# A written-out order of some 3,300 pieces of work laid out anew on one core: pairwise attention, sparse gathers and layernorms

## The chip, the cores and the metric

The kernel runs on one core of a Trainium2 chip. The metric is the device time of one execution in microseconds (us), lower is better. Each of the core's engines (PE for matmuls, DVE for vectors, ACT for functions, POOL for gathers, SP for the other transfers) works through its own list of instructions strictly in the order in which the kernel emits them, and waits where an instruction needs another engine's result.

## The reference

All sizes are 3327 nodes by 256 features, float32. `adj` is sparse (each entry is there with probability 0.0024, and the diagonal always).

```python
h = relu(layernorm(x))
# layer 0, two steps
R = adj + eye;  R = R / R.sum(-1, keepdims=True)
Z = 0;  Xf = Xa = h
for n in range(2):
    A  = top_p_attention(Xa, W1, W2, W3)       # softmax(q k^T), the largest until 0.9 of the mass, renormalised
    Xf = R @ Xf
    Xa = A @ Xa
    Z  = Z + Xf @ U1[n].T + Xa @ U2[n].T
x = x + layernorm(h + Z) * ln_g + ln_b
# layer 1
h = relu(layernorm(x))
D = (adj.sum(1) + 1e-9) ** -0.5
x = x + relu((D[:, None] * adj * D[None, :] @ h) @ W.T + b)
```

## The kernel before

**Blocks and stages.** The nodes lie in 26 blocks of 128 rows, the last with 127. A start stage normalises all nodes, and makes keys, queries and the products of h with the weights, which it stores in HBM (`gb_hbm`). Then follow step 0 (`ATT_0`, `LISTING`, `FIRST`), step 1 (`ATT_1`, `SECOND`) and the late layer (`LATE`, `WHOLE`).

**A block of attention** (kinds `ATT_0`, `ATT_1`) goes over all 3327 columns: logits on PE (`lg0`, `lg1`, L866), exponentials on ACT (`ex0`, `ex1`, L883), then a search for the threshold by small steps and whole passes on ACT (`guess`, `ev1s`, `ev2s`, L897, L927), or for the first block or two by DVE (`w_over`, L934), set by `BY_VECTOR`. DVE then takes a window of the candidates (`win`, L1049), finds the largest of each stretch (`wm`, L1056), sorts the best 40 (`sort`, L1066 and L1069: MAX8, then MATCH_VALUE_LOAD and MATCH_REPLACE8, ten times), finds the cut, in step 1 marks the kept ones (`match`, L1109), and drops all others (`drop`, L1114). PE transposes the result in seven groups (`tr`, L1128), ACT copies them (`atc`, L1134), and PE multiplies them with the nodes (`att`, L1143). In step 0 `attend` (L1149), `xtk_t`, `xtk_c`, `k_m` and `k_c` (L814) then make the block's share of the keys of step 1; a step's first attention needs the keys of all blocks of the step before. In step 1 the block ends with residuals, two layernorms and the store of hn (`resid`, `input2`, `node2`, `stn`; L1254, L1258, L1273, L1288).

**Sparse products.** `LISTING` finds, for each block of rows, the nodes that its part of adj names, and lays the places of their columns into `a_idx` (L667) and their numbers into `v_idx`. From these POOL gathers 8 tiles of adj (`ga`, L678) and 8 tiles of nodes (`gv`, L692) by indirect DMA, each 128 rows; PE multiplies tile by tile (`adj0` to `adj7`, `adj_gathered`, L702). In step 0 (`FIRST`) the nodes come from gb_hbm and the products give y; in step 1 (`SECOND`) from y_hbm and give hz, which lies in HBM until the block's residual. In the late layer 18 blocks (`LATE`) gather 8 tiles of hn each, and 8 blocks (`WHOLE`: 0, 4, 7, 10, 13, 16, 19, 22) are done densely with 26 matmuls (L1554) in a part `first` and a part `second`: 25 and 1 for blocks 0 and 4, 13 and 13 for the others. In all POOL issues 768 gathers: 416 in step 0, 208 in step 1, 144 late.

**Buffers.** The gathered nodes go to 16 tiles in a ring: `gather_node` takes the tile that has been free longest, `adj_gathered` gives it back behind its matmul. There are 4 tiles for gathered adj, 3 for the attention's rows (`e`) and 2 for hz.

**What sets the order.** Nothing is scheduled by a compiler. Each piece of work (an `att2`, a `gv5`, a `sort3`) gets a number, and `Plan.run` emits the pieces sorted by it:

```python
places = PLACES[kind] | MOVED.get((kind, i), {})
at = BASES[kind] + PERIODS[kind] * (i if n is None else n) + (SHIFTS[kind][i] if kind < len(SHIFTS) else 0.0)
for name, piece in do.items():
    plan.add(at + places[name], piece)
```

The numbers are written by hand or by an earlier search. They look like times but are only sort keys: an engine starts each instruction as soon as the one ahead of it allows and what it reads is there. `PLACES` holds the places of one kind's pieces within a block, `PERIODS` the distance from block to block, `MOVED` a block's own places, and `EVENTS` the places of single pieces (the centring of the keys: `keys` for step 0, `centre` for step 1).

Of the kernel before, what the change touches and what calls it, by code (L numbers as in the profile page):

```python
# [105 lines left out]
BASES = (-1.892, 870.475, -13.053, -5.69, 853.823, -80.36, 1720.169, 1724.788)  # L106
PERIODS = (30.0573, 29.8334, 30.2195, 29.6001, 29.4593, 1.6, 11.4611, 29.3857)
# [11 lines left out]
        ldq=-44.287, lg0=-38.973, ex0=-25.597, lg1=-20.538, ex1=-16.452, guess0=-16.41, guess1=-16.131,  # L119
        guess2=-15.977, guess3=-15.603, guess4=-14.457, guess5=-14.33, guess6=-12.806, guess7=-12.277, ev1r=-11.76,  # L120
        ev1s=-8.469, st10=-7.961, guess8=-7.057, st11=-6.906, st12=-5.943, st13=-4.39, st14=-3.503, st15=-3.334,
        st16=-1.613, st17=0.027, thr=0.214, st18=0.892, win=3.72, cut0=7.309, wm1=9.04, wm0=10.134, wm3=10.495,
        wm2=12.344, sort0=14.201, sort1=14.201, sort2=15.126, sort3=16.348, sort4=16.684, sort5=17.022, sort6=18.245,
        sort7=18.909, sort8=19.469, sort9=19.668, cut1=19.862, cut2=20.795, cut3=21.407, cut4=22.022, cut5=22.834,
        drop=23.642, tr0=26.604, atc0=29.007, tr2=31.084, att0=32.223, atc2=32.504, tr1=33.541, atc1=35.266,
        inv=37.184, tr3=38.707, att1=40.1, tr4=41.126, atc3=41.825, att2=42.068, tr5=43.428, atc4=44.771,
        atc5=46.924, att3=47.519, tr6=48.685, atc6=50.691, att4=50.866, att5=51.309, edge=51.319, att6=52.006,
        attend=54.3, xtk_t=56.039, xtk_c=58.125, k_m=61.105, cut6=61.775, k_c=62.744, q_c=63.484, xu_m=65.976,
        xu_c=67.312, stxt=75.943, stq=77.565, stxu=81.473,
    ),  # L130
    dict(
        ldq=-120.275, lg0=-63.07, lg1=-47.295, ex0=-46.566, ex1=-41.634, guess0=-41.061, guess1=-39.487,
        guess2=-38.859, guess3=-38.65, guess4=-38.64, guess5=-37.462, guess6=-37.063, ev1s=-36.233, half=-35.672,
        mass0=-35.413, ev1r=-35.055, mass1=-32.043, tail0=-31.473, tail1=-31.053, tail2=-30.763, tail3=-28.525,
        mass2=-28.221, st10=-26.599, st11=-25.175, st12=-24.135, aux2=-23.815, ev2s=-21.461, st13=-18.043,
        btw1=-17.852, st14=-15.208, aux0=-14.988, aux1=-14.22, sec10=-12.922, sec11=-12.131, sec12=-10.743,
        thr=-7.89, sec13=-7.788, nt2=-2.992, win=2.783, wm2=6.046, wm0=6.444, wm1=6.454, wm3=6.526, sort0=8.121,
        sort1=8.162, sort2=9.437, sort3=10.527, sort4=11.217, sort5=12.023, sort6=12.773, sort7=13.564, sort8=15.249,
        cut0=15.328, sort9=15.348, cut1=16.458, cut2=17.341, cut3=18.102, cut4=18.886, cut5=19.961, match=21.123,
        drop=23.999, tr0=28.827, atc0=29.172, tr4=29.605, tr1=32.779, att0=32.801, tr2=32.803, atc1=33.007,  # L140
        att1=33.809, atc4=34.739, tr3=34.759, atc2=36.727, att2=37.933, tr5=38.539, tr6=39.45, atc3=40.18,
        att3=40.29, ldx=44.319, atc5=45.361, atc6=45.991, ldh=48.128, att4=48.571, inv=49.727, att5=50.339,
        att6=51.666, resid0=55.38, resid1=57.694, resid2=60.354, root1=64.136, xbet=66.296, input20=67.759,
        input21=69.483, edge=70.892, input22=73.309, input23=75.045, root2=79.569, node2=90.831, stn=94.821,
    ),
# [7 lines left out]
        store=12.996,  # L153
# [1634 lines left out]
```

## Time and profile before

| what | value |
|---|---|
| median of 11 runs | 1647.92 us (1646.08 to 1651.88) |
| the profiled execution's own time | 1650.14 us |
| its span | 1648.4 us |
| mean granted TensorE clock | 0.966 |
| PE busy | 1487.4 us (90%) |
| DVE busy | 1300.0 us (79%) |
| ACT busy | 1137.7 us (69%) |
| POOL busy | 1039.0 us (63%) |
| first gather starts | 95.56 us |
| last gather of step 0 starts | 771.45 us |
| first window of step 1 starts | 811.21 us |
| last drop of step 1 starts | 1421.91 us |
| first and last gather of hn start | 1450.38 and 1629.75 us |

The span is the time from the first to the last instruction on the chip. An engine's share is over the whole span. A row of a timeline has the start in us, the duration, the engine, the line of the kernel, the operation, what it writes and reads, and in brackets how long the engine stood idle ahead of it and what released it; "issue" means that nothing which the profile shows was waited for.

### The profile page before, as it was taken

How to read it: one execution, taken by the hardware profiler on the slowest of the kernel's cores; microseconds unless marked ns; L12 is line 12 of the kernel's file. 1: busy time of each engine (PE TensorE's matmuls, PEld its weight loads, DVE VectorE, ACT ScalarE, POOL GpSimd, SP SyncE). 2: the span in 40 equal slices, each digit the busy share in tenths (PEclk: the TensorE clock that was granted, in tenths of full speed). 3: DMA queues.
4: the chain of work that ended last, by engine and by line, in shares of the span. 5: the costliest groups of instructions: out<-in, count | busy, mean ns of one | idle time of the engine just before them, and what ended most of it. 6: DMA issues, size and time to landing. Idle time of an engine off the chain costs nothing.

```text
span 1648.4 us, 24872 instructions
## 1 busy us (share of the span) xinstructions
PE 1487.4 (90%) x7372; PEld 1161.8 (70%) x7372; DVE 1300.0 (79%) x3965; ACT 1137.7 (69%) x2692; POOL 1039.0 (63%) x808
## 2 busy tenths in 40 slices
PE   5958999989999999999499999999999998899996
PEld 3526777767777777777277777777777777788884
DVE  5589999779999997964599999999999999611111
ACT  3666887657777776872889999999999997200000
POOL 0058888788888887885566454566666562067774
PEclk9969999989999999999699999999999999999998
DMA  6556867657557766444533432343344334377764
GB/s 189 171 182 206 266 209 229 187 174 227 171 170 219 220 196 182 151 143 128 183 102 117 128 116 87 119 128 111 100 125 128 114 116 134 98 236 267 264 196 120
DMA packets 149167, 272.26 MB, mean 165 GB/s; under 512 B 29603, under 2 KB 94496, under 8 KB 148000
## 3 DMA queue, kind: packets, MB, share of 16 engines
q1 hardware_dynamic: 109456, 181.58, 33.8%
q0 software_dynamic: 33536, 87.08, 19.0%
q10 hardware_dynamic: 6032, 1.93, 0.5%
q8 instruction: 60, 0.98, 0.2%
q14 instruction: 83, 0.68, 0.1%
HBM read 221.08 MB, written 49.41 MB: 164 GB/s over the span
## 4 chain that ended last, share of the span: by engine, by line
PE 37%; DVE 27%; issue 11%; ACT 10%; DMA 6%; POOL 3%; SPq 0%; DVEq 0%; POOLq 0%; ACTq 0%
PE att_acc L1143 13%; DVE cand L1056 6%; DVE w L1109 5%; PE late_sums L1554 5%; PE adj_acc L702 4%; PE p_t L1128 4%; PE p_l L866 4%; PE late_acc L702 3%; DVE e L1114 3%; ACT e L883 3%; ACT ja L927 2%; DMA vg<-hn_hbm,v_idx 2%; DMA vg<-gb_hbm,v_idx 2%; DVE cand L1069 2%; DVE val L1066 2%
## 5 line engine op out<-in xcount | busy, mean ns | idle before, releaser
L692 POOL DMA_INDIRECT vg<-y_hbm,v_idx x208 | 326.1, 1568 | 254.0 <-PE adj_acc L702 192.0
L927 ACT ACTIVATE ja<-e,t 128x3327 uint8<-128x3327 f32 x127 | 389.6, 3068 | 0.7
L678 POOL DMA_INDIRECT ac<-in_adj_t,a_idx x208 | 276.5, 1329 | 146.9 <-DVE own L619 83.8
L1143 PE MATMUL att_acc<-h,at 128*128 128x256 f32 (+1 forms) x1352 | 323.6, 386 | 0.0
L1143 PE MATMUL att_acc<-xa,at 128*128 128x256 f32 (+1 forms) x1352 | 321.8, 382 | 0.0
L692 POOL DMA_INDIRECT vg<-gb_hbm,v_idx x208 | 273.9, 1317 | 63.4 <-issue 45.4
L1143 PEld LDWEIGHTS att_acc<-h,at 128*128 128x128 f32 (+1 forms) x1352 | 253.3, 193 | 40.7 <-issue 7.6
L1143 PEld LDWEIGHTS att_acc<-xa,at 128*128 128x128 f32 (+1 forms) x1352 | 253.2, 192 | 31.2
L1134 ACT COPY at<-p_t 128x512 f32<-128x512 f32 (+1 forms) x364 | 197.1, 545 | 110.7 <-PE p_t L1128 104.5
L1128 PE MATMUL p_t<-ident,e 128*128 128x128 f32 x1352 | 211.8, 283 | 51.8 <-DVE e L1114 38.0
L1128 PEld LDWEIGHTS p_t<-ident,e 128*128 128x128 f32 x1352 | 164.4, 145 | 110.7 <-DVE e L1114 41.1
L1056 DVE MAX8 cand<-w 128x8 f32<-128x208 f32 x832 | 238.6, 359 | 0.2
L702 PE MATMUL adj_acc<-vg,ac 128*128 128x257 f32 (+1 forms) x832 | 231.1, 391 | 8.5 <-DMA vg<-gb_hbm,v_idx 5.7
L866 PE MATMUL p_l<-kt,q 64*128 64x512 f32 (+1 forms) x832 | 183.7, 556 | 30.1 <-ACT e L883 28.0
L1049 DVE SCALAR_TENSOR_TENSOR w<-e,t 128x3327 f32<-128x3327 f32 x52 | 191.1, 3675 | 21.3 <-ACT t L897 21.0
L883 ACT ACTIVATE e<-p_l 128x2048 f32<-128x2048 f32 x104 | 161.6, 1554 | 18.2 <-PE p_l L866 15.9
L702 PEld LDWEIGHTS adj_acc<-vg,ac 128*128 128x128 f32 x832 | 149.3, 193 | 34.0 <-issue 8.3
L692 POOL DMA_INDIRECT vg<-hn_hbm,v_idx x144 | 136.5, 948 | 54.9 <-issue 36.7
L866 PEld LDWEIGHTS p_l<-kt,q 64*128 64x128 f32 x832 | 75.1, 193 | 113.3 <-issue 67.4
L730 ACT COPY xt_k<-p_turn 128x256 f32<-128x256 f32 x52 | 19.0, 369 | 152.8 <-PE p_turn L726 151.3
L570 DVE TENSOR_REDUCE most<-adj_sb 128x7 f32<-128x896 f32 x104 | 105.2, 1012 | 6.3 <-DMA adj_sb<-in_adj_t 5.4
L1114 DVE SCALAR_TENSOR_TENSOR e<-w,kept,e 128x3327 f32<-128x3327 f32 x26 | 96.7, 3719 | 0.1
(397 smaller groups left out, 2102.2 us busy)
## 6 DMA issues: line engine op xcount, KB each, us to landing
ac<-ac_hbm SPq DMA_DIRECT2D x70, 512.0 KB
adj_sb<-in_adj_t SPq DMA_DIRECT2D x78, 448.0 KB
ac_hbm<-ac SPq DMA_DIRECT2D x26, 512.0 KB
adj_row<-in_adj_t SPq DMA_DIRECT2D x8, 1664.0 KB
adj_sb<-in_adj_t SPq DMA_DIRECT2D x26, 320.0 KB
gb_hbm<-gb SPq DMA_DIRECT2D x26, 256.0 KB
gb<-gb_hbm SPq DMA_DIRECT2D x26, 256.0 KB
q<-q_hbm SPq DMA_DIRECT2D x104, 32.0 KB
```

Of the source, the lines that this page charges most:

```text
L678: nc.gpsimd.indirect_dma_start(s["list"][:, k, :], None, adj_rows, bass.IndirectOffsetOnAxis(ap=s["a_idx"][:, k : k + 1], axis=0))
L692: nc.gpsimd.indirect_dma_start(t[:, :D], None, hbm[:, :], bass.IndirectOffsetOnAxis(ap=v_idx[:, i, k : k + 1], axis=0))
L702: nc.tensor.matmul(s["acc"][:, :width], s["ac"][:, k, :], rows[:, :width], start=(k == 0), stop=(k == SLOTS - 1))
L866: nc.tensor.matmul(pl[:, at : at + cw], s["q"][rows, :], kt[rows, c0 + c : c0 + c + cw], start=True, stop=True)
L883: nc.scalar.activation(halves(s["e"])[:, :, c0 : c0 + w], logits_of(s.pop(("l", g)))[:, :, :w], AF.Exp, accum_out=s["zp"][:, g : g + 1],)
L927: nc.scalar.activation(junk, s["e"][:, :N], f, bias=s["t"], scale=-1.0, accum_out=s[name])
L1049: nc.vector.scalar_tensor_tensor(w[:, :N], ev, s["t"], ev, op0=ALU.is_le, op1=ALU.mult, accum_out=s["below"])
L1056: nc.vector.max(s["cand"][:, 8 * n : 8 * n + 8], s["w"][:, c0 : c0 + cw])
L1114: nc.vector.scalar_tensor_tensor(ev, kept, kept8[:, step * NB + i, 0:1], ev, op0=op, op1=ALU.mult, accum_out=den)
L1128: nc.tensor.transpose(pt[:, c : c + P], s["e"][:, b * P : (b + 1) * P], ident)
L1134: nc.scalar.copy(at[:, :w], pt[:, :w])
L1143: nc.tensor.matmul(s["att"][:, :D], at[:kb, c : c + P], v[b][:kb, :D], start=(b == 0), stop=(b == NB - 1))
```

## The change

Only the numbers of the order change. All instructions stay; they are emitted in another sequence. `PLACES` and `SHIFTS` are new throughout, and the first and last blocks of each step (0, 1, 25 of step 0; 0, 1, 2, 25 of step 1), some blocks of `FIRST`, `SECOND` and `LATE`, and all of `WHOLE` have places of their own in `MOVED`. In step 0 gathers of adj and of nodes take turns in shorter runs, and the products of `FIRST` lie later by about a block against the attention. In step 1 more of a block's sorting stands in one piece on DVE. In the late layer block 2 is gathered ahead of block 1, with their products in the old sequence. Two functions read a value one `yield` later, since a piece that writes it now may come after.

```diff
-BASES = (-1.892, 870.475, -13.053, -5.69, 853.823, -80.36, 1720.169, 1724.788)
-PERIODS = (30.0573, 29.8334, 30.2195, 29.6001, 29.4593, 1.6, 11.4611, 29.3857)
+BASES = (-1.219, 870.817, -13.308, 19.745, 850.288, -80.36, 1723.434, 1717.681)
+PERIODS = (30.0457, 29.8979, 30.2735, 28.5613, 29.0638, 1.6, 11.5234, 30.9119)
 ATT_0, ATT_1, LISTING, FIRST, SECOND, START, LATE, WHOLE = range(8)
...
-        gv3=36.873, gv6=37.71, gv1=38.549, gv0=39.478, gv5=41.654, gv2=42.696, lda=49.308, ldg=49.654, gv4=49.849,
-        gv7=50.182, adj0=50.797, adj1=50.94, adj2=53.03, adj3=56.206, adj4=57.968, adj5=59.203, adj6=62.128,
-        adj7=63.299, roots=65.636, prop=66.557, mixy=74.549, stxf=84.692,
+        gv1=5.282, gv2=21.832, gv7=24.204, gv6=26.685, lda=38.398, gv0=42.53, gv3=45.834, gv5=49.994, adj0=53.488,
+        gv4=54.175, adj1=54.407, adj2=56.475, adj3=58.925, ldg=60.866, adj4=61.154, adj5=61.417, adj6=63.064,
+        adj7=64.895, prop=68.892, roots=69.299, mixy=79.436, stxf=81.479,
...
     (6, 1): dict(
-        load=-179.07, gath=0.428,
+        load=-105.361, gath=8.668,
     ),
     (6, 2): dict(
-        load=-69.885, gath=9.897,
+        load=-54.284, gath=-3.365,
     ),
...
     (7, 7): dict(
-        row=-166.823, first=-44.325, second=-34.048, m=-27.848, turn=-18.413, mt=-15.792, out=-14.297, ldx=-2.972,
-        add=13.779, st=17.888,
+        row=-174.561, first=-143.338, second=-36.982, ldx=-23.235, m=-22.339, turn=-7.269, mt=-2.182, out=-1.77,
+        add=4.041, st=35.074,
     ),
...
 EVENTS = dict(
-    keys=-32.591, centre=764.748, roots=817.644, hn=827.229, nodes=878.278, last_nodes=918.935, hn_last=1606.3,
+    keys=-34.222, hn=759.96, centre=779.44, nodes=800.108, roots=866.959, last_nodes=881.044, hn_last=1387.109,
 )
...
     def step_0(s):
+        rest = fma("rest", s["z"], 1.0 - TOP_P, s["over"])
+        yield
         sign = s["sign"]
-        rest = fma("rest", s["z"], 1.0 - TOP_P, s["over"])
-        yield
         below = fma("below_n", sign, -0.5, value[AIM[0] - 0.5 * N])
...
     def input_2(i, t):
-        hz, x, n = t["hz"], t["x"], t["n"]
+        hz, n = t["hz"], t["n"]
         nc.vector.scalar_tensor_tensor(hz, hz, n["mv"][:, 0:1], gam, op0=ALU.subtract, op1=ALU.mult)
         yield
+        x = t["x"]
         nc.vector.scalar_tensor_tensor(x, hz, n["rr"], x, op0=ALU.mult, op1=ALU.add)
```

## The prediction, made before the changed kernel ran

> **What bounds the kernel now.** I read the windows first, because the whole-span shares mix three stages with three different limits. Columns: window, its length, then busy time and instructions of PE, PEld, DVE, ACT, POOL, and the granted clock, DMA share and GB/s.
>
> ```profile
> 600.00:630.00 30.00, 28.79 (x151) 22.91 (x149) 21.62 (x75) 23.13 (x55) 24.45 (x19) 1.00 0.66 210
> 780.00:810.00 30.00, 17.02 (x72) 10.30 (x70) 9.53 (x17) 24.95 (x59) 15.79 (x12) 0.78 0.48 153
> 990.00:1020.00 30.00, 27.76 (x141) 22.27 (x139) 29.58 (x81) 28.47 (x67) 11.37 (x13) 1.00 0.35 104
> 1590.00:1620.00 30.00, 28.80 (x138) 24.43 (x137) 6.68 (x15) 2.60 (x7) 22.69 (x25) 1.00 0.62 189
> ```
>
> POOL's 24.45 looks like room, but 19 gathers have 0.30 us of issue ahead of each: 24.45 + 19 x 0.30 = 30.2. In step 0 POOL never rests. The last row is the same case: 22.69 + 25 x 0.30 = 30.2. In step 1 (third row) DVE is full and POOL is not. Between steps (second row) nothing is full: there one chain of short steps sets the time.
>
> The timeline of POOL and DVE shows what a gather costs:
>
> ```profile
> 757.43 0.95 POOL L692 DMA_INDIRECT vg<-gb_hbm,v_idx  x1 [0.30 <-PE att_acc L1143]
> 758.68 3.71 POOL L692 DMA_INDIRECT vg<-gb_hbm,v_idx  x1 [0.30 <-issue]
> ...
> 757.88 3.68 DVE L1114 SCALAR_TENSOR_TENSOR e<-e,kept 128x3327 f32<-128x3327 f32 x1
> ```
>
> A gather's pitch is 0.95 + 0.30 = 1.25, but one that meets a 3.7 us DVE instruction (w_over, window, drop) stays until that ends. From 95.6 to 772.4 the trace holds step 0's 416 gathers with no gap over 0.45: 416 x 1.25 = 520, and 53 long ones add 154, sum 674, against 676.8 elapsed. The 53 are 26 windows, 26 drops and one w_over.
>
> Between the steps:
>
> ```profile
> 766.09 1.23 PE L702 MATMUL adj_acc<-vg,ac 128*128 128x257 f32 x2 [2.79 <-DMA vg<-gb_hbm,v_idx]
> ...
> 784.74 0.47 ACT L1149 ACTIVATE xa<-att_acc,inv 128x256 f32<-128x256 f32 x1 [2.46 <-PE att_acc L1143]
> 787.40 0.36 ACT L814 ACTIVATE kt<-p_kq,km 64x127 f32<-64x127 f32 x1
> ...
> 811.21 3.67 DVE L1049 SCALAR_TENSOR_TENSOR w<-e,t 128x3327 f32<-128x3327 f32 x1
> ```
>
> Block 25's drop ends at 761.5. PE then stands before FIRST(24)'s last product, for a gather; FIRST(25) lies among block 25's att matmuls. The last keys (kt) are there at 787.4, and 23.8 later step 1's first window starts.
>
> **The change, part by part.** Both kernels issue the same instructions; only their order on each engine differs, so the sum is one of waits. It is made against the profiled execution (1650.14; span 1648.4 and 1.7 around it), 2.2 above the median of the runs.
>
> *Start.* The first gather (95.56) waits for a_idx(0) on DVE. In the new order four chunk reductions lie between the centring of the keys and a_idx(0), before it one. Three more at 1.01 (L570's mean) cost 3.0, less about 0.4 because part lay elsewhere ahead of it: +2.6 (0 to +4).
>
> *Step 0.* The runs are shorter (369 runs of one kind instead of 306), but POOL's work is the same 520 + 154: as many gathers, and as many long DVE instructions. An in-order queue that is never idle gains nothing from order. PE's pauses here are slack beside POOL. It could lose if a gather found no free tile of 16; by the new order each tile comes free over 10 us ahead of its next gather. 0.
>
> *Between the steps.* FIRST(24)'s products now stand between att3 and att6 of block 25, and FIRST(25)'s behind (1,0)'s second logit group. So PE transposes as soon as the drop ends (761.5) and does 26 x 2 att records at 0.2165 (11.3), 26 transposes at 0.108 (2.8) and 8 products (3.5), 17.6 in all, to about 779 to 780 instead of 784.6; FIRST(25)'s three small ACT instructions (0.7) leave the path to kt. Worked through, kt comes near 780: -7.5, from 0 (another gather ends last) to -14 (no copy on ACT is waited for). y(25) is stored later, but y gathers have 231 us of gaps in step 1.
>
> *Step 1.* DVE is the bound, so its order has a price. The timeline of block 25's sorting shows it:
>
> ```profile
> 1414.16 0.29 DVE L1066 MAX8 val<-cand 128x8 f32<-128x128 f32 x1
> 1414.38 0.14 DVE L1103 TENSOR_TENSOR edge<-pre,thr 128x1 f32<-128x1 f32 x1
> ...
> 1414.88 0.29 DVE L1066 MAX8 val<-cand 128x8 f32<-128x128 f32 x1
> 1415.21 0.09 DVE L1069 MATCH_VALUE_LOAD cand<-val,cand 128x8 f32 x1
> 1415.29 0.28 DVE L1069 MATCH_REPLACE8 cand<-val,cand 128x128 f32<-128x128 f32 x1
> 1415.48 0.42 DVE L442 BATCH_NORM_STATS2 bn_st<-x_in 128x6 f32<-128x256 f32 x1
> ```
>
> A MAX8 whose next neighbour reads its output holds that neighbour back 0.33; with another instruction between, 0.22. Fitted over all pitches of step 1, a dependent neighbour costs 0.117. The old order has 134 such pairs from the first window of step 1 to its last match, the new one 231: the sorts run more in one piece, no longer between other blocks' small steps. 97 x 0.117 = +11.3, less 2.7 for pairs two apart: DVE's floor rises from 602.3 to 611.3. The old stretch took 610.5, so it held 8.2 of waits. If the new order has none, +0.8; with the same waits, +9. I take +6.8, nearer the upper end, because the rows with waits (t from ACT, L897) have no shorter path in the new order.
>
> The Trainium skill weighs against this term. Its page "VectorE: DVE Perf Modes", section "The DRAIN you can't avoid", says that after every DVE instruction the next starts only when the pipe is empty, whether or not the two are chained. By that, order would cost nothing and this term would be 0 or less; the rows' 0.22 against 0.33 say otherwise.
>
> *End of step 1.* Block 7's first dense part (13 matmuls, 5.6) now stands on PE just ahead of block 25's transposes. Of its 5.6, 2.4 fill the pause that PE has there (1425.74) and some 1.1 smaller pauses ahead of it; up to +2.1 is left, and hz's last load lies better by 1.5: +0.6 (-1.5 to +2.1).
>
> *Late layer.* Rows, with S = 1450.38 the first hn gather:
>
> ```profile
> 1450.38 0.96 POOL L692 DMA_INDIRECT vg<-hn_hbm,v_idx  x1 [11.07 <-issue]
> ...
> 1510.56 0.95 POOL L692 DMA_INDIRECT vg<-hn_hbm,v_idx  x1 [0.30 <-issue]
> ...
> 1508.27 3.62 PE L702 MATMUL late_acc<-vg,ac 128*128 128x256 f32 x16
> ...
> 1629.75 0.95 POOL L692 DMA_INDIRECT vg<-hn_hbm,v_idx  x1 [0.30 <-issue]
> ```
>
> 144 gathers at 1.252 reach to 1630.7 without a gap. Gather 49 (block 9's first, 1510.56) takes the tile that block 6's first product frees, and that product starts at 1508.27: in time by under 2. In the new order block 2 is gathered before block 1, but PE still multiplies block 1 first, so PE stands until gather 16 has landed: issued at S + 15 x 1.252 = S + 18.8, ended 0.95 later, landed 2.45 after its issue-end (766.09 against 763.64 above), S + 22.2; product done S + 22.6 instead of S + 15.7. From there to block 6's product PE has five dense halves (D7, D10, D13, D10, D13: 28.2), products 2, 3, 5 (10.4), D0's last matmul (0.4), and turns and outputs (6.1): 45.1, so S + 67.7, its first pair S + 68.1. Gather 49 is due at S + 60.1: POOL stands 8.0, most in one gap. As POOL is full to the end, and the 17.7 from its last gather to the end of the span stay, +7.9 (0 if PE does its dense halves earlier than worked out; +10 with the wait of 0.85 at block 8 and a product more).
>
> Sum: 2.6 + 0 - 7.5 + 6.8 + 0.6 + 7.9 = +10.4 on 1650.14, which is 1660.5 in the profiled execution and 1658.3 as median.
>
> On PE's pauses, which the new order does shorten between the steps: the clock was 0.78 and 0.65 in 780 to 810 and 810 to 840, and 1.00 in most of both steps. The Trainium skill's page "TensorE: Matmul & The Clock Gate", Part 1, puts the clock down to half after one window of about 3.4 us without work. By that rule fewer pauses would gain; but PE's share of the chain there is 23 us (761.5 to 784.6), and the clock of 750 to 780 was 0.94: at most 23 x 0.06 = 1.4 us, so it does not turn the sum.
>
> **The rivals.** *Faster: DVE's floor does not rise.* If the 97 pairs cost nothing because the new neighbours fall where DVE would have waited for ACT anyway, and the 8.2 of waits go, step 1 gives -8.2 instead of +6.8: 1658.3 - 15.0 = 1643.3. For it: ACT's 28.47 of 30 leaves DVE waits to fill. Against: DVE's 29.58 leaves 0.4 in 30. It decides where step 1's pitch (drop to drop 23.76) falls below 23.4. A bigger gain between the steps (attention a whole block ahead of the gathers, -18) would go the same way: with it, 1633.
>
> *No change:* the late gap does not open because PE enters the late layer with more dense work behind it: 1658.3 - 7.9 = 1650.4, and with half the rise of step 1 1647. It decides at gather 49.
>
> *Slower still: step 1 gets a wait of its own.* hz is loaded closer to its use and SP's queue is one line for all loads; 0.3 us in each of 25 blocks adds 7.5: 1666; with the upper end of the late layer 1668. For it: resid0(25) waited 11.5 for hz in the old order already. Against: in other blocks the new order leaves about 8 us between store and load.
>
> **How the numbers follow.** My forecast (1652 to 1662) has 0.42, slower still 0.18, no change 0.13, the faster rival with its bigger variant 0.27. About 0.2%, 3.3 us, is what can be told from no change: faster means under 1644.6, slower over 1651.2. From the cases: faster 0.27, same 0.13, slower 0.60. The range leaves out a tenth at each end: 1637, between 1633 and 1643, and 1672, a bit above the slower rival because several of my lower bounds rest on places worked out by hand.
>
> **What would show it.** First gather near 98 (start). Still no POOL gap in step 0, or the "nothing from order" step is wrong. kt copy near 780 counted from the old start, first window 23.8 behind it. Drop-to-drop pitch near 24.0. A gap of about 7 on POOL 60 us after the first hn gather, 17.7 from the last gather to the end. If the pitch is 23.5 or less, or gather 49 comes without a gap, the forecast is wrong.

## The result, and the profile after

The changed kernel takes 1688.7 us (median of 8 runs, 1684.42 to 1691.47) against 1649.24 for the kernel before (31 runs): a ratio of 1.0237, 95% interval 1.0225 to 1.0250. It is slower, as forecast, but by 39 us where the sum said 10.4, and the time lies above the range of 1637 to 1672. The profiled execution has a span of 1687.4 against 1648.4. In some runs both kernels, the one before included, took some 13% longer; these stand only in the list at the end of the experiments, and no conclusion rests on them.

The span can be cut at the places that the prediction named. All numbers are from the two profiled executions, in us; "of it new" is what a stage adds to the delay that it was handed.

| place | before | after | difference | of it new | forecast |
|---|---|---|---|---|---|
| first gather starts | 95.6 | 100.8 | +5.2 | +5.2 | +2.6 |
| last drop of step 0 starts | 757.9 | 765.6 | +7.7 | +2.5 | 0 |
| first window of step 1 starts | 811.2 | 822.6 | +11.4 | +3.7 | -7.5 |
| from there to the last match | 610.6 | 623.8 | | +13.2 | +6.8 |
| first hn gather starts | 1450.4 | 1473.6 | +23.2 | -1.4 | +0.6 |
| hn gathers, first to end of the last | 180.3 | 196.2 | | +15.9 | +7.9 |
| last gather to the end of the span | 17.7 | 17.6 | | -0.1 | 0 |

The column "of it new" adds up to the 39.0 by which the span grew. Every stage but the end of step 1 and the tail lost more than forecast, and the stage that should have gained, between the steps, lost.

The windows of the kernel after, with the columns of before (window, its length, then busy time and instructions of PE, PEld, DVE, ACT and POOL, the granted clock, DMA share, GB/s):

```profile
600.00:630.00 30.00, 29.38 (x158) 23.35 (x157) 24.53 (x74) 20.48 (x51) 21.45 (x18) 1.00 0.65 207
795.00:825.00 30.00, 14.90 (x61) 8.38 (x62) 13.70 (x26) 26.81 (x70) 0.00 (x0) 0.83 0.36 107
990.00:1020.00 30.00, 28.34 (x144) 22.18 (x141) 29.23 (x77) 28.66 (x61) 18.03 (x9) 1.00 0.29 90
1590.00:1620.00 30.00, 27.02 (x115) 22.54 (x114) 4.31 (x10) 1.67 (x5) 22.69 (x25) 0.90 0.76 251
```

In this stretch of step 0 (first row) POOL is no longer full: 21.45 + 18 x 0.30 = 26.9 of 30. That holds for two parts of step 0 only, up to about 340 and from 580 to 640; in the rest of it POOL has no such gap. PE's 29.38 is of this stretch alone. Over the bulk of step 0 PE is not busier than before (kernel before, then after):

```profile
190.00:760.00 570.00, 538.58 (x2803) 426.71 (x2802) 499.98 (x1637) 419.87 (x1038) 463.04 (x352) 0.99 0.62 190
190.00:760.00 570.00, 536.28 (x2786) 425.47 (x2786) 505.64 (x1647) 423.41 (x1059) 449.47 (x344) 0.98 0.61 188
```

DVE's 29.23 in step 1 (third row) and POOL's 22.69 with 25 gathers in the late layer (last row) are close to those of before: what was lost there lies elsewhere than in these rows, in step 1 mostly in its first blocks, in the late layer mostly ahead of 1550.

**Step 0.** The timeline of POOL shows gathers that stand, which before had none over 0.45. (In brackets: how long the engine stood, and what released it.)

```profile
148.79 0.94 POOL L759 DMA_INDIRECT ac<-in_adj_t,a_idx  x1 [5.36 <-PE att_acc L1224]
194.10 0.94 POOL L759 DMA_INDIRECT ac<-in_adj_t,a_idx  x1 [4.92 <-DMA ac_hbm<-ac]
600.73 0.94 POOL L773 DMA_INDIRECT vg<-gb_hbm,v_idx  x1 [6.05 <-PE adj_acc L783]
```

The first is the first gather of adj of block 2. In brackets the view names PE, but the indices that this gather reads (`a_idx`) came from DVE only at 148.03; before they were there 15 ahead of it. DVE's row and the gather before, then DVE's row after:

```profile
129.72 0.16 DVE L667 TENSOR_SCALAR a_idx<-a_row 128x8 int32<-128x8 f32 x1
144.87 0.94 POOL L678 DMA_INDIRECT ac<-in_adj_t,a_idx  x1 [0.30 <-issue]
```

```profile
147.86 0.17 DVE L748 TENSOR_SCALAR a_idx<-a_row 128x8 int32<-128x8 f32 x1 [0.21 <-DVE there L659]
```

So most of this stand, up to 148.03, is for the indices. The second gathers adj, too, and stands for one of the 4 tiles (`ac`), until a store of an older tile has ended. The third gathers nodes and stands until a product of `FIRST` has read its tile. Over the normal 0.30 of issue, POOL's gaps in step 0 sum to 24.0, before to 2.0. POOL's way from first to last gather grew by 10.6 only, since its gathers stood less on long DVE instructions: beyond 0.95 each they took 143.8 in sum, before 155.2. The drops run 15.6 late in block 24 (743.09 against 727.50), and block 25 makes up 7.8 of it; that is why the row of the last drop shows no more than +2.5. The product for which the third stands was late for a reason of its own, on PE:

```profile
595.90 0.61 PE L709 MATMUL p_shared<-nodes,own 128*128 128x12 f32 x4 [2.67 <-ACT at L1215]
596.36 3.53 PE L1224 MATMUL att_acc<-h,at 128*128 128x256 f32 x8
600.29 1.89 PE L1224 MATMUL att_acc<-h,at 128*128 128x256 f32 x8
```

After a stand of 2.67, eight att records took 3.53, the next eight 1.89. In the ten microseconds from 594 the granted clock was 0.83 on average.

**The start.** The timeline of DVE ahead of the first gather:

```profile
90.04 1.08 DVE L651 TENSOR_REDUCE most<-adj_sb 128x7 f32<-128x896 f32 x1
...
96.96 0.16 DVE L721 TENSOR_TENSOR which<-own_no,lent 128x2 f32<-128x2 f32 x1 [3.10 <-ACT lent L716]
...
98.96 1.08 DVE L651 TENSOR_REDUCE most<-adj_sb 128x7 f32<-128x896 f32 x1
...
100.36 0.17 DVE L748 TENSOR_SCALAR a_idx<-a_row 128x8 int32<-128x8 f32 x1
```

The reductions of the next block stand ahead of a_idx, as forecast. On top DVE stands 3.10 for ACT's `lent`, before 0.80, which the forecast did not contain.

**Between the steps**, from the timelines of PE, ACT and DVE:

```profile
770.61 1.03 PE L1224 MATMUL att_acc<-h,at 128*128 128x256 f32 x4
...
776.24 0.61 PE L841 MATMUL p_kq<-xt_k,wkq 128*128 128x128 f32 x4
776.69 0.60 PE L1209 MATMUL p_t<-ident,e 128*128 128x128 f32 x4
777.68 1.13 PE L1294 MATMUL p_xu<-u,xt_k 128*128 128x256 f32 x4 [0.39 <-ACT q_s L878]
...
787.84 1.99 PE L947 MATMUL p_l<-kt,q 64*128 64x512 f32 x8
...
792.02 2.76 PE L1224 MATMUL att_acc<-h,at 128*128 128x256 f32 x12
```

```profile
794.81 0.47 ACT L1230 ACTIVATE xa<-att_acc,inv 128x256 f32<-128x256 f32 x1 [2.97 <-PE att_acc L1224]
797.57 0.36 ACT L895 ACTIVATE kt<-p_kq,km 64x127 f32<-64x127 f32 x1 [0.80 <-PE p_kq L841]
```

Block 25's drop ends at 769.3. PE hardly pauses from then to block 25's last att matmul, which is what the change was forecast to do. Yet xa comes 25.5 after the drop's end, and before it came 23.2 after it (784.74 less 761.56). PE is full with more than was counted: the rest of block 24 (att at 770.61, its keys at 776.24, its share of Z at 777.68), the first logits of step 1 (787.84) and 24 records of `FIRST` ahead of block 25's last att.

**Step 1**, the waits of DVE from the first window to the last drop (line, what it waited for: us in total, times, longest):

```profile
DVE tail_d L1057 <- ACT mass L978: 2.8, 3, 1.5
DVE prop L1248 <- PE adj_acc L783: 2.4, 1, 2.4
DVE shift L1365 <- ACT rd L978: 2.2, 3, 1.1
DVE x_in L1357 <- ACT bn_rr L511: 1.6, 1, 1.6
```

With three smaller ones they sum to 10.4; the same view of the kernel before sums to 3.2. Of the 10.4, 7.2 lie between the first drop and 958, in the first five blocks. The drops run late by 11.3 in block 0, 19.1 in block 5 and 24.7 in block 25.

**The late layer**, timelines of PE and POOL:

```profile
1492.26 0.70 PE L783 MATMUL late_acc<-vg,ac 128*128 128x256 f32 x2 [1.50 <-DMA vg<-hn_hbm,v_idx]
1495.68 3.78 PE L783 MATMUL late_acc<-vg,ac 128*128 128x256 f32 x8 [2.73 <-DMA vg<-hn_hbm,v_idx]
1499.26 1.06 PE L1636 MATMUL late_sums<-hn_last,adj_row 128*128 128x256 f32 x2
...
1506.82 3.41 PE L783 MATMUL late_acc<-vg,ac 128*128 128x256 f32 x15
```

```profile
1507.69 0.94 POOL L773 DMA_INDIRECT vg<-hn_hbm,v_idx  x1 [4.35 <-PE late_acc L783]
...
1546.78 0.94 POOL L773 DMA_INDIRECT vg<-hn_hbm,v_idx  x1 [7.15 <-PE late_acc L783]
```

Of blocks 1 and 2, PE multiplies block 1 first, whose rows are now gathered last, and stands three times for them. Behind the last stand 8 records take 3.78, while before 16 took 3.62; from 1495 to 1500 the granted clock was 0.50. Block 2's product starts only at 1506.82, 33.2 after the first hn gather, and gather 25 stands for the tile that it frees. Gather 49 stands 7.15 at 73.2 after the first. All gaps of the late layer sum to 15.8 over the 0.30, before to 1.0.

### The profile page after: what moved, and what is told of

Read it like the earlier page. It is cut to its first block, busy times and chain, and to the rows that moved or that the text cites. A ratio compares the mean times of both kernels' runs of the same rounds, so it can differ in the third digit from the quotient of the medians.

```text
span 1687.4 us, 24906 instructions
## 1 busy us (share of the span) xinstructions
PE 1503.4 (89%) x7372; PEld 1167.3 (69%) x7372; DVE 1309.4 (78%) x3965; ACT 1140.5 (68%) x2692; POOL 1024.9 (61%) x808
## 4 chain that ended last, share of the span: by engine, by line
PE 38%; DVE 28%; ACT 15%; issue 11%; DMA 5%; POOL 1%; ACTq 0%; SPq 0%; DVEq 0%; POOLq 0%
PE att_acc L1224 13%; DVE cand L1137 7%; ACT ja L1008 7%; DVE w L1190 4%; PE adj_acc L783 4%; PE p_t L1209 4%; PE late_sums L1636 4%; PE late_acc L783 4%; PE p_l L947 3%; DVE e L1195 3%; PE p_gb L857 2%; ACT e L964 2%; DVE cand L1150 2%; DVE val L1147 2%; ACT at L1215 2%
## 5 line engine op out<-in xcount | busy, mean ns | idle before, releaser
L773 POOL DMA_INDIRECT vg<-y_hbm,v_idx x208 | 314.2, 1511 | 155.9 <-PE adj_acc L783 67.1
L759 POOL DMA_INDIRECT ac<-in_adj_t,a_idx x208 | 256.3, 1232 | 162.6 <-DVE own L700 89.4
L1224 PE MATMUL att_acc<-h,at 128*128 128x256 f32 (+1 forms) x1352 | 327.9, 388 | 3.0 <-ACT at L1215 3.0
L773 POOL DMA_INDIRECT vg<-gb_hbm,v_idx x208 | 282.7, 1359 | 75.3 <-issue 38.4
L1224 PEld LDWEIGHTS att_acc<-xa,at 128*128 128x128 f32 (+1 forms) x1352 | 248.6, 191 | 49.8 <-ACT at L1215 10.1
L1209 PE MATMUL p_t<-ident,e 128*128 128x128 f32 x1352 | 202.1, 279 | 47.9 <-DVE e L1195 21.2
L783 PE MATMUL adj_acc<-vg,ac 128*128 128x257 f32 (+1 forms) x832 | 223.6, 390 | 12.3 <-DMA vg<-y_hbm,v_idx 9.8
L1209 PEld LDWEIGHTS p_t<-ident,e 128*128 128x128 f32 x1352 | 159.6, 142 | 94.0 <-ACT at L1215 29.2
L964 ACT ACTIVATE e<-p_l 128x2048 f32<-128x2048 f32 x104 | 161.5, 1553 | 17.6 <-PE p_l L947 13.7
L1349 POOL TENSOR_TENSOR x_in<-x_in,bet 128x256 f32<-128x256 f32 x26 | 32.3, 1243 | 174.3 <-DMA x_in<-in_x 116.0
```

The source lines that it names most:

```text
L759: nc.gpsimd.indirect_dma_start(s["list"][:, k, :], None, adj_rows, bass.IndirectOffsetOnAxis(ap=s["a_idx"][:, k : k + 1], axis=0))
L773: nc.gpsimd.indirect_dma_start(t[:, :D], None, hbm[:, :], bass.IndirectOffsetOnAxis(ap=v_idx[:, i, k : k + 1], axis=0))
L783: nc.tensor.matmul(s["acc"][:, :width], s["ac"][:, k, :], rows[:, :width], start=(k == 0), stop=(k == SLOTS - 1))
L964: nc.scalar.activation(halves(s["e"])[:, :, c0 : c0 + w], logits_of(s.pop(("l", g)))[:, :, :w], AF.Exp, accum_out=s["zp"][:, g : g + 1],)
L1209: nc.tensor.transpose(pt[:, c : c + P], s["e"][:, b * P : (b + 1) * P], ident)
L1224: nc.tensor.matmul(s["att"][:, :D], at[:kb, c : c + P], v[b][:kb, :D], start=(b == 0), stop=(b == NB - 1))
```

## The experiments

An edit here exchanges places between the two kernels: the pieces named get the places that they have in the other kernel, all else stays.

**1. The changed kernel once more**, no edit.

> The changed kernel as it is, a second time, beside the kernel before on the same chip, as the measure for the exchanges of single stages, in whose runs both kernels took some 13% longer than in the first runs. If those 13% fall on both kernels alike, the ratio is 1.024 again. If they come from something that the order changes too (engines that stand without a wait that the profile shows), the ratio is another one, between 1.00 and 1.02, and the exchanges must be read by their traces' stages, not by their totals.

Measured: 1687.92 us, ratio 1.0220 (1.0190 to 1.0250). First window at 824.1, stretch of step 1 626.1, late gathers 193.2. The stages are thus good to some 3 us each, and readings of 1 or 2 us from one trace are not worth an argument. The old order spreads as much: experiments 3 to 6, with the old start, have their first gather at 95.9 to 97.1 (before 95.6; with the new start 99.6 to 100.9), and experiments 4 and 6, which change nothing ahead of it, have the first window at 814.7 and 813.0 (before 811.2).

**2. The changed kernel with block 1 gathered before block 2 in the late layer.** Only two numbers exchange their places (6 is `LATE`, then the block; the places as they come out):

```diff
-    (6, 1): gath at 1732.102     (6, 2): gath at 1731.592
+    (6, 1): gath at 1731.592     (6, 2): gath at 1732.102
```

> The new order with one exchange: block 1's eight hn gathers ahead of block 2's, as their products are. Theory (PE's stand before block 1's product, and the slow matmuls behind that stand, start all the gaps): POOL's gaps in the late layer, 15.8 us in sum, fall to about 5, with one of about 3.5 left at gather 49; from first to last hn gather about 186 us instead of 196; some 10.5 us less than the new order, a ratio of about 1.017. Rival (the dense halves of blocks 10 and 13 ahead of block 6's product are the cause by themselves): the gap at gather 49 takes over most of what the others had, no more than 5 us are won, a ratio of 1.020 or more.

Measured: 1679.31 us, ratio 1.0167 (1.0139 to 1.0195). The hn gathers take 185.5 instead of 196.2, their gaps sum to 5.2 instead of 15.8. Timelines of PE and POOL of this kernel:

```profile
1489.68 3.62 PE L788 MATMUL late_acc<-vg,ac 128*128 128x256 f32 x16
...
1540.04 0.95 POOL L778 DMA_INDIRECT vg<-hn_hbm,v_idx  x1 [4.82 <-PE late_acc L788]
```

Block 1's product is one run of 16 records at full rate, with no stand for a DMA. One gap is left, at gather 49. So the exchange of the two gathers alone costs 10.7 of the 15.9 that the late layer lost (7.7 against the 193.2 of experiment 1), the time at half rate included. The gap that is left comes where dense halves stand on PE ahead of block 6's product; experiment 3 moves one of them.

**3. Step 0 all old, step 1 new, and the late layer mended further.** Start stage, `LISTING`, `FIRST` and `ATT_0` at the old places, the exchange of experiment 2, and one dense half later (7 is `WHOLE`):

```diff
-    (7, 13): second at 1773.75
+    (7, 13): second at 1778.98      # behind block 6's product
```

> Three things at once, each read by its own stage: START, LISTING, FIRST and ATT_0 in their old sequence; step 1 new; in the late layer block 1's gathers ahead of block 2's and the second dense half of block 13 (5.6 us of PE) put behind block 6's product. Theory: first window of step 1 back at 811 instead of 822.6 (step 0 loses by its own order); first to last drop of step 1 still 606 to 608 (step 1 loses by its own order, whatever step 0 hands over); from first to last hn gather 180.5 to 181 with no gap at gather 49, since the 4.8 left by the exchange alone are less than 5.6. Total about 1662, a ratio of 1.008. Rivals: the first window stays at 819 or later (the first blocks of step 1 in their new places make it late); the stretch of step 1 falls to 596 or less (it was slow because the new step 0 handed its y over late); the gap at gather 49 stays above 3 (another wait than block 6's product).

Measured: 1665.45 us, ratio 1.0103 (1.0082 to 1.0125). The first window came at 813.7: 2.5 after that of before, 8.9 ahead of that of the changed kernel. Kernels with nothing changed up to there reach 814.7 (named in experiment 1), so the order of the start and of step 0 accounts for the late first window, and nothing beyond the spread is left for the new places of step 1's first block. From first to last drop step 1 took 604.4, against 593.9 before and 607.3 in the changed kernel: behind the old step 0, step 1 is slow as well. That refutes the rival that its loss is an echo of a late step 0. DVE's waits here sum to 8.1.

The later dense half did not help. Gather 49's gap went, but others opened behind it, as POOL's timeline shows:

```profile
1554.48 1.10 POOL L888 DMA_INDIRECT vg<-hn_hbm,v_idx  x1 [1.97 <-PE late_acc L898]
...
1586.53 0.94 POOL L888 DMA_INDIRECT vg<-hn_hbm,v_idx  x1 [1.25 <-PE late_acc L898]
```

The late gathers took 184.4, 1 less than in experiment 2. PE is full there: the half's time went from the way to block 6's product to the ways of later ones.

**4. The kernel before, with the sorts of step 1 in one piece.** This takes the suspected cost alone and makes it bigger:

```diff
-        sort1=8.162, sort2=9.437, sort3=10.527, sort4=11.217, sort5=12.023, sort6=12.773, sort7=13.564, sort8=15.249,
-        cut0=15.328, sort9=15.348, ...
+        sort1=8.131, sort2=8.132, sort3=8.133, sort4=8.134, sort5=8.135, sort6=8.136, sort7=8.137, sort8=8.138,
+        cut0=15.328, sort9=8.139, ...
```

> The kernel before with one edit: in step 1 each block's ten sorting steps stand in one piece on DVE (sort1 to sort9 right behind sort0), all else where it was. Pairs of neighbours on DVE of which the second reads the first's output go from 134 to 306 between the first window and the last match of step 1. Theory (each costs 0.117 us where DVE is full): DVE's floor for that stretch goes from 602.3 to 620.8, and the stretch from 610.6 to between 621 (no waits left) and 629 (the waits of before on top); a ratio of 1.006 to 1.011. Rival (the pairs are covered, since DVE would have waited for ACT anyway, or the price is not real): the stretch stays within 4 us of 610.6 and the ratio within 0.002 of 1.

Measured: 1678.19 us, ratio 1.0166 (1.0144 to 1.0188). Nothing but nine numbers was changed, no instruction was added, and step 1's stretch grew from 610.6 to 634.2, by 23.6, more than the 629 that the theory allowed at most. DVE's timeline of this kernel shows how:

```profile
1019.41 0.29 DVE L1066 MAX8 val<-cand 128x8 f32<-128x128 f32 x1
1019.74 0.09 DVE L1069 MATCH_VALUE_LOAD cand<-val,cand 128x8 f32 x1
1019.81 0.28 DVE L1069 MATCH_REPLACE8 cand<-val,cand 128x128 f32<-128x128 f32 x1
1020.12 0.29 DVE L1066 MAX8 val<-cand 128x8 f32<-128x128 f32 x1
```

The instruction behind these MAX8 reads its result and starts 0.33 after it; that is so for 104 of the 130 in step 1, before for 32. DVE's waits sum to 4.0, 0.8 more than before, so 22.8 is left for 172 more pairs of dependent neighbours (306 instead of 134): 0.133 a pair. That order alone costs time on DVE is thereby shown.

The Trainium skill's section "The DRAIN you can't avoid" (page "VectorE: DVE Perf Modes") says that the next instruction starts when the pipe is empty, but adds: "A next op that is not held starts earlier". The rows shown with the prediction and here agree with the addition: a neighbour that does not read the MAX8's result starts 0.22 after it, while it still runs (0.29), and one that reads it starts at 0.33.

**5. Opening old.** Start stage and blocks 0 to 10 of step 0 (`LISTING`, `ATT_0`, `FIRST`) at the old places, blocks 11 to 25 new; step 1 and the late layer (`ATT_1`, `SECOND`, `LATE`, `WHOLE`) old.

> START and blocks 0 to 10 of LISTING, FIRST and ATT_0 in their old sequence, blocks 11 to 25 of step 0 new; step 1 and the late layer old. Theory (step 0's loss is made in its opening, by the later first gather and the gathers that stand for tiles of adj, and the later blocks give back 3 us): at block 11 the drop lies at 409 as before, the last drop of step 0 at about 755, the first window of step 1 between 808 and 814 instead of 822.6, the ratio between 0.998 and 1.003. Rival (the later blocks lose too, once they no longer follow a late start: products of FIRST that lag by a block hold PE): the last drop of step 0 at 762 or later, the first window at 817 or later, a ratio of 1.004 or more.

Measured: 1665.77 us, ratio 1.0087 (1.0070 to 1.0104). Step 0's last drop starts at 756.2, where the changed kernel has 765.6 and the kernel before 757.9. POOL's two early stands, for `a_idx` and for a tile of adj, are gone from its trace; those for node tiles are not: for products of `FIRST` POOL waited 19.5 in all here and 19.7 in the changed kernel. So the old opening gives the last drop 9.4 back, more than its whole delay. It does not follow that the later blocks lose nothing: block 24's drop is still 6.1 later than before (733.62 against 727.50), in the changed kernel 15.6, and block 25 makes up 7.8 in both. The first window came at 814.8, a little later than expected, as in experiments 4 and 6. After it step 1 lost 11 more in one place between its blocks 0 and 1, which the waits of DVE name:

```profile
DVE prop L1392 <- PE adj_acc L927: 13.6, 2, 12.4
```

The old first blocks of step 1 multiply y early, and the new end of step 0 has y late. The two do not fit together, and this time belongs to neither kernel. By it the ratio lies above the 1.003 of the theory.

**6. Fewer pairs.** In the kernel before, 133 small pieces of step 1 were moved by a few places so that they come between dependent neighbours, 134 pairs becoming 105, to see whether the price works the other way and beats both kernels. In block 10, for one:

```diff
-    (1, 10): edge=1241.541, node2=1261.48, resid0=1226.029, resid2=1231.003
+    (1, 10): edge=1242.504, node2=1258.517, resid0=1227.826, resid2=1233.207
```

> The kernel before with some 160 small pieces of step 1 moved by at most 6 of the order's units, none of those that wait for PE (propagation, residual) to an earlier place, so that they stand between two instructions on DVE of which the second reads the first's output. Such pairs go from 134 to 105 between the first window and the last match of step 1. Theory (a pair costs 0.12 to 0.14 us where DVE is full): 29 x 0.12 to 29 x 0.14 = 3.5 to 4.1 us less, the stretch 607 instead of 610.6, a ratio of 0.9975. Rival (what the moved pieces save comes back as waits): within 1.5 us of before, a ratio within 0.001 of 1, or above.

Measured: 1704.66 us, ratio 1.0315 (1.0292 to 1.0338), where a small gain was expected. Its waits of DVE in step 1:

```profile
DVE tail_d L1014 <- ACT mass L935: 21.7, 13, 3.6
DVE more L1059 <- ACT ja L965: 10.1, 6, 2.0
DVE den_s L1064 <- ACT size_s L935: 9.4, 9, 1.9
```

The moved pieces (node2, inv, resid and others) feed ACT. 14 of the 19 moved node2 stand 2.7 to 5.6 units later. In them ACT reads `shift` from DVE, and ACT's waits of the same stretch show what that does:

```profile
ACT hn_adj L1322 <- DVE shift L1321: 17.1, 4, 7.6
ACT kt L1322 <- DVE shift L1321: 15.8, 6, 5.6
```

With three more such rows ACT stands 51.3 for `shift`, before 8.7. ACT goes through its list in order, so it stands there ahead of the next block's search, and DVE then waits for the search. All of DVE's waits sum to 54.8, 51.6 more than before, and the way from first to last drop grew by 50.5. The pairs are a small price beside that. No kernel of this study beat the one before.

**7. The other runs**, beside a kernel before of 1850 to 1871 us. Only their ratios are listed, and nothing is concluded from them.

The changed kernel with the late layer at its old places (1.0105):

> The new order with the late layer (LATE and WHOLE) in its old sequence. Theory (each stage's loss is its own): the gaps of POOL behind the first hn gather close, and the run takes 1688.7 - 15.9 = about 1673. Rival (the late layer loses because of the state in which step 1 hands over, with a dense half already done and hn stored later): POOL still has gaps of over 5 us in the late layer, and the run stays above 1680.

The exchange of experiment 2 (1.0083, and in a second run 1.0035):

> The new order with one exchange: block 1's eight hn gathers ahead of block 2's, as their products are. Theory (PE's stand before block 1's product, and the slow matmuls behind that stand, start all the gaps): block 1's product starts 14.5 us after the first hn gather and ends at 18 instead of 25.8; the gaps at gathers 25, 33 and 41 go, the one at gather 49 shrinks from 7.2 to about 3.5; 1688.7 - 10.5 = about 1678. Rival (the dense halves of blocks 10 and 13 ahead of block 6's product are the cause by themselves): the gap at gather 49 stays 7 or more in sum with the ones before it, and the run takes 1684 or more.

> The new order with one exchange: block 1's eight hn gathers ahead of block 2's, as their products are. Theory (PE's stand before block 1's product, and the slow matmuls behind that stand, start all the gaps): the gaps at gathers 25, 33 and 41 go, the one at gather 49 shrinks from 7.2 to about 3.5 us; about 10.5 us less than the new order, a ratio of about 1.0175 to the kernel before. Rival (the dense halves of blocks 10 and 13 ahead of block 6's product are the cause by themselves): the gap at gather 49 takes over most of what the others had, and no more than 5 us are won, a ratio of 1.021 or more.

The changed kernel with the start and step 0 at their old places (1.0068, 1.0047 and 1.0055):

> The new order with START, LISTING, FIRST and ATT_0 in their old sequence, step 1 and the late layer new. Theory (step 0 is lost in step 0): the first gather is back at about 96, POOL has no gap over 0.5 in step 0, the first window of step 1 is back at about 811 instead of 822.6, and the run takes 1688.7 - 11.4 = about 1677. Rival (the first blocks of step 1 in their new places are what makes the first window late): the first window stays at 819 or later and the run at 1685 or more.

> The new order with START, LISTING, FIRST and ATT_0 in their old sequence, step 1 and the late layer new. Theory (step 0 is lost in step 0): the first gather is back at about 96, POOL has no gap over 0.5 in step 0, the first window of step 1 is back at about 811 instead of 822.6; 11.4 us less than the new order, a ratio of about 1.017. Rival (the first blocks of step 1 in their new places are what makes the first window late): the first window stays at 819 or later, a ratio of 1.021 or more.

> The new order with START, LISTING, FIRST and ATT_0 in their old sequence, step 1 and the late layer new, run again by itself beside the kernel before. Theory (step 0 loses by its own order): first gather back at about 96, no POOL gap over 0.5 in step 0, first window of step 1 at about 811 instead of 822.6; 11.4 us less than the new order, a ratio of about 1.017. Rival (the first blocks of step 1 in their new places make the first window late): first window at 819 or later, a ratio of 1.021 or more.

The kernel before with the new step 1 (1.0123):

> Only step 1 new: START, LISTING, FIRST, ATT_0, LATE and WHOLE in their old sequence, ATT_1 and SECOND new. Theory (step 1's own order costs what step 1 lost, 24.29 instead of 23.76 from drop to drop): the stretch from first to last drop of step 1 stays at about 607 instead of 594 us, the late layer has no gap at gather 49, and the ratio is about 1.007. Rival (step 1 was slow because the new step 0 handed its last y over late): the stretch falls back below 598 and the ratio is within 0.002 of 1.

An earlier choice of pieces for experiment 6 (1.0427):

> The kernel before with 166 small pieces of step 1 (residuals, normalisation steps, the sums of SECOND, the edges) moved by at most some 6 of the order's units, so that they stand between two instructions on DVE of which the second reads the first's output. Such pairs go from 134 to 98 between the first window and the last match of step 1. Theory (a pair costs 0.12 to 0.14 us where DVE is full): 36 x 0.12 to 36 x 0.14 = 4.3 to 5.0 us less, the stretch from first window to last match 606 instead of 610.6, a ratio of 0.997. Rival (the moved pieces bring as much waiting as they save, or the other engines hold step 1 at its length): within 1.5 us of before, a ratio within 0.001 of 1, or above.

One edit did not give what it was for, the changed kernel with step 1 and the late layer old (5.266). Its first logits of step 1 lay ahead of the centring of the keys that they read, and it went the kernel's general path, for inputs that the fast one doesn't fit, in 9831 us:

> The new order with ATT_1 and SECOND in their old sequence, step 0 and the late layer new. Theory (DVE's order is what step 1 loses by): drop to drop falls from 24.29 to about 23.8, the stretch from the first drop to the last from 607.3 to about 594, and the run takes 1688.7 - 12 = about 1677. Rival (step 1 is slow because the y gathers start 34 us later, after the new step 0): the stretch stays above 603 and the run above 1685.

The last question, which part of the opening makes the loss, went to the changed kernel with the start and only blocks 0 to 2 of step 0 old (1.0069, 1.0046 and 1.0106):

> The new order with START and only blocks 0 to 2 of LISTING, FIRST and ATT_0 in their old sequence. Theory (what the first blocks lose, 5.3 us at the first gather and 11.8 at block 2's drop, is carried to the end of step 0): first gather at 96, block 2's drop within 3 us of 172.9, the last drop of step 0 at 755 to 759 instead of 765.6, first window of step 1 at 811 to 816, a ratio of 1.016 to 1.020. Rival (blocks 3 to 10 lose by themselves and settle at the same lag, whenever they start): the last drop of step 0 at 763 or later and the ratio at 1.021 or more.

> The changed kernel, with the start stage and the first three blocks of step 0 (attention, listing and sparse products) at the old places; from block 3 of step 0 on all is new. With the opening's first eleven blocks old, the last drop of step 0 started at 756.2 instead of 765.6. Theory: that gain comes from the start and blocks 0 to 2, where the first gather is late (100.8 instead of 95.6) and the gathers of adj stand for a free tile: last drop of step 0 at 755 to 759, first window of step 1 at 812 to 817, time 9 below that of the changed kernel, near 1679, ratio 1.018. Rival: only the 5.2 of the first gather come back, and blocks 3 to 10 lose the rest again: last drop at 760 to 763, first window at 817 to 820, time near 1684, ratio 1.021.

> The changed kernel, with the start stage and the first three blocks of step 0 (attention, listing and sparse products) at the old places; from block 3 of step 0 on all is new. With the opening's first eleven blocks old, the last drop of step 0 started at 756.2 instead of 765.6. Theory: that gain comes from the start and blocks 0 to 2, where the first gather is late (100.8 instead of 95.6) and the gathers of adj stand for a free tile: last drop of step 0 at 755 to 759, first window of step 1 at 812 to 817, time 9 below that of the changed kernel, near 1679, ratio 1.018. Rival: only the 5.2 of the first gather come back, and blocks 3 to 10 lose the rest again: last drop at 760 to 763, first window at 817 to 820, time near 1684, ratio 1.021.

In the last of them the last drop of step 0 starts at 906 us, which neither theory's numbers can be held against. Whether the opening's loss lies in blocks 0 to 2 or 3 to 10 stays open.

## Why the prediction was right and wrong

The direction was right, and so were the mechanisms of the two largest losses, pairs on DVE and the late gathers. The sizes were not, and one stage had the wrong sign: the kernel lost almost four times what the sum said. The sum was short by 28.6, which is 16.3 up to the first window of step 1, 6.4 in step 1, 8.0 in the late layer, and -2.1 in the end of step 1 and the tail.

*Start* (+2.6, measured +5.2): the four reductions were there; the 3.10 that DVE stands for `lent`, 2.3 more than before, was not looked for. The upper bound of +4 fell too, in this pair of traces; over all of them the new start loses 2.6 to 5.4.

*Step 0* (0, measured +2.5 to the last drop, +10.6 to the end of the gathers): the runs of one kind went from 134 to 222 there (306 and 369 count block by block and take in step 1's gathers). The step failed at "it could lose if a gather found no free tile of 16". The forecast asked the right question, but only of the 16 node tiles. Two other things that a gather waits for were left out: its indices (the stand of 5.36) and the 4 tiles of adj (4.92). Its answer was wrong for the node tiles as well, as the stand of 6.05 shows. Why the margin of over 10 us was gone there is not worked out; PE's stand of 2.67 and the 1.6 more for eight records at half rate account for 4.3 of it. "An in-order queue that is never idle gains nothing from order" was true and one-sided: it can lose.

*Between the steps* (-7.5, measured +3.7): the biggest miss. The step that failed is "17.6 in all". The forecast counted block 25's 52 att records, 26 transposes and 8 products. On PE's list from the drop to xa there also stand the end of block 24 (att 0.9, turn 0.4, keys 0.6, Z 1.1), the first logits of step 1 (2.0), 8 more records of products (1.7) and p_mean (0.4). These make 7.1, and 17.6 + 7.1 = 24.7, against the 25.5 from the drop's end to xa; most of what is left is in the transposes, 3.7 with their pauses where the forecast had 2.8. That PE's stand for a gather went was right; work took its place. This makes 2.3 of the +3.7. Another 1.2 lies between kt and the window (25.0, before 23.8), but experiments 4 and 6, with the old order up to there, have 25.4 and 25.2 as well, so it can't be put down to the change.

*Step 1* (+6.8, measured +13.2): two terms. For the order alone the forecast had +9.0 (its floors, 602.3 and 611.3; its own sum, 11.3 - 2.7, is 8.6); the trace has 13.2 - 7.2 of added waits = 6.0. The three other kernels with the new step 1 give 5.6 to 7.3 by the same subtraction (stretches 626.1, 622.9 and 621.1; waits 12.0, 8.2 and 8.1). With 97 pairs that is 0.06 to 0.08 a pair, less than the 0.117 that was fitted and the 0.133 of experiment 4. The single pair was not cheaper: behind a sort's MAX8 a dependent neighbour starts 0.325 after it and another one 0.211 after it, before 0.327 and 0.206, and the 53 more dependent ones among them make 6.4 already. All other neighbours together come out near nothing, new pairs against neighbours that follow each other closer; the forecast had allowed 2.7 for pairs two apart. What it set against this term from the Trainium skill (page "VectorE: DVE Perf Modes", section "The DRAIN you can't avoid") left out the addition quoted in experiment 4. The other term has the wrong sign: the forecast let 2.2 of 8.2 old waits go, of which the trace names only 3.2, and 7.2 came. They are what the rival "step 1 gets a wait of its own" described, but for ACT's `mass` and `bn_rr` and PE's product, not for hz, and most of it in the first five blocks. hz was not waited for there although its load is issued 1.7 to 6.2 behind its store in all blocks but one, not about 8 as the forecast had it. What in the new order makes them was not tried; they come behind the old step 0 too (8.1 in experiment 3).

*End of step 1* (+0.6, measured -1.4): within its range.

*Late layer* (+7.9, measured +15.9): the mechanism was right, block 1's product waiting for the gathers of block 1, and experiment 2 shows it. The tile that PE waits for last was there 22.1 after the first hn gather, forecast 22.2. The mis-sized term is what follows it, "product done S + 22.6": 8 records were left, not 2, and they ran at half rate, so it was done at 25.9. Block 2's product was then late for gather 25 already, where the forecast had the first stand at gather 49. That one stood 7.15, forecast 8.0, which is partly luck: block 6's product started 72.3 after the first gather instead of 67.7, and gather 49 was itself some 6 late by the stands ahead of it. Gathers 25 and 41 and smaller ones add the rest.

*The clock* was weighed for the stage between the steps alone and dropped. In the late layer it cost 1.9 on the 8 records and 0.5 on each of the next two groups (1.06 against 0.59, and 1.26 against 0.76 in experiment 2), 2.9 in all in this trace. The Trainium skill's page "TensorE: Matmul & The Clock Gate", section "HAM oscillation — how this bites in real kernels", describes a related case: bursts of matmuls of about 2 us, with waits of some 3 to 5 us for DMA between them that are longer than a window of about 3.4 us, so that the clock falls before every burst. Here the waits were 0.85, 1.50 and 2.73, with bursts of 0.70 between them, no single one as long as that window, and the clock was still 0.93 on average from 1490 to 1495 and 0.50 from 1495 to 1500. PE, moved onto a late producer, paid for the wait and then again for the slow restart.

## What to carry to other kernels

When the order of a queue changes, ask of every ring of buffers that it writes to, the small ones first, when each tile comes free in the new order, and of every index that it reads, when that is written; a queue that is full before has only time to lose. Gather in the order in which you multiply: one exchanged pair of blocks cost 8 to 11 us, and its first stand moved into later gathers (25, 33, 41, 49) through the ring. And where a pause is taken off an in-order engine, sum all that stands on its list up to the instruction that counts, other blocks' pieces included, before you call the pause a gain.

## What the runs showed of the hardware

Nine changed numbers that put DVE's sorts in one piece cost 22.8 us over 172 pairs of dependent neighbours, 0.133 a pair, without a new instruction; behind a sort's MAX8 (0.29 long) a neighbour that reads its result starts 0.33 after it, another one 0.21. PE ran at half rate (8 records in 3.53 and 3.78 instead of 1.89) after a stand of only 2.67 in step 0 and three of 0.85, 1.50 and 2.73 in the late layer. A gather that meets a 3.7 us DVE instruction stays on POOL until that ends, and a POOL that stands meets fewer of them: POOL's gaps in step 0 grew by 22.0, its way from first to last gather by 10.6.
